# One graph layer pair on one core: the last unit's one-hot rows in its gather buffer, the adjacency sums in five parts over four PSUM banks

## The chip, the core and the metric

The kernel runs on one core of one Trainium2 chip. The metric is the device time of one execution in microseconds; the median of three runs of the kernel before is 566.61 us (565.72 to 568.6).

## What is computed

Two graph layers are applied to x (4096 nodes, 64 features) with an adjacency matrix adj of 4096 x 4096 zeros and ones, about eight ones in a row. Both are pre-norm residual layers:

```
h = relu(layernorm(x))
# layer 0: hyperbolic aggregation over the neighbours j of each node i
log_ij = logmap(h_i, h_j)                 # on the Poincare ball
agg_i  = sum_j adj_ij / deg_i * log_ij
x      = x + expmap(0, agg @ W0 + b0)     # tanh of a norm
# layer 1: the neighbours in order of their column, each weighs half of the next
h   = relu(layernorm(x))
w   = adj * 0.5 ** (k - pos)              # pos: rank of the neighbour in its row
out = x + w @ (h @ W1) + b1
```

## The kernel before

The nodes are 32 blocks of 128 (a partition each). The work has three streams, all written into one list of steps with a due time each (`plan`, filled by `at`, L1454 to L1548); the steps are issued in that order and a list scheduler then fixes the order of the instructions on each engine. [...]

**The adjacency** is loaded block by block (L879, 64 MB in all), transposed on TensorE (L888) and copied by ScalarE as fp8 weights into four `masks` (L891), one for each quarter p of the rows. From them come the candidate lists of each row (`pack`, `search`, `tail_*`), and in place the weights of layer 1 (`step`, L1412).

**Layer 0** goes by 17 units (L1490). Unit n below 16 has two blocks of ordinary neighbour slots (2 x 6 gathers); units 5 to 16 have also a tail: the rows' further neighbours of two or three blocks, three gathers for a block. So unit 16, the last one, has a tail alone (blocks 30 and 31, six gathers). For a unit, `fetch` loads the block's own rows (L1117, L1126), `gather` (L1139) issues one indirect DMA of 128 rows for each slot on GpSimd, `tail_rows` builds one-hot rows (L1156, L1163), transposes them (L1169), copies them (L1170) and selects the target rows by matmuls (L1178). `differ` (L1192 to L1222), `weigh` (L1234 to L1251) and `total` (L1261 to L1288) work out the weighted difference vectors, and the matmuls of L1266 with `total_tail` (L1295) add the tails to y. The tiles of the pool `blk` have one buffer each: the one-hot rows `oh`, the tile `mr` (transposed one-hot rows, target rows, and later the weighted one-hot rows), d and w. So the rows of unit n+1 wait until unit n's total has read `mr`. The gather tile `g` has two buffers.

**Between the layers** `middle` takes five groups of blocks (L846: 8, 8, 8, 6 and 2 blocks) in four stages: stage 0 scales y (L1327 to L1330), stage 1 multiplies by W0 (L1302, L1345), stage 2 does tanh, residual and layernorm (L1353 to L1359, L711 at its end), stage 3 multiplies by W1 and writes the result in three bf16 pieces side by side into `sup` (L1386, L1390, L1403, L1405).

**Layer 1** is the sum over the node blocks: for a part c of the blocks (`sums`, L848) and two row blocks (p, n), `collect` runs one matmul for each node block and row block into a PSUM tile of two halves (L1422, last part also L1430), and adds the tile, whose 192 columns are the three pieces, to `acc`. There are 16 pairs (p, n) for each part. Two ways lead out of PSUM:

- the VectorE way: a reduction over the three pieces (L1441) and one scaled addition to `acc` (L1445)
- the GpSimd way: ScalarE copies the tile to SBUF (L1436, tile `dg` or `mr` in turn by n), and GpSimd adds the three pieces to `acc` one after the other (L1438)

Before, the first part takes the VectorE way, the second and third take the GpSimd way, the last one is split half and half by n. All collects share the two PSUM buffers of `ps_a`. `write` (L1451) sends four blocks of `acc` out after the last part. Part c can start when the groups named in its entry are through stage 3.

```
groups = [(0, 8), (8, 8), (16, 8), (24, 6), (30, 2)]
sums = [(0, 16, (0, 1)), (16, 7, (2,)), (23, 6, (3,)), (29, 3, (4,))]
pool = 0 < c < len(sums) - 1 or (c == len(sums) - 1 and n >= 2)
o = ps_a.tile([P, 2, 2 * P], F32, name="a_ps")
ev = (lst if n % 2 else blk).tile([P, 2, W3], F32, name="dg" if n % 2 else "mr")
```

A dense version of the kernel follows under a condition (L1568) that this input does not meet.

Of the kernel before, what the change touches and what calls it, by code (L numbers as in the profile page):

```python
# [11 lines left out]
F32 = mybir.dt.float32  # L12
BF16 = mybir.dt.bfloat16
# [6 lines left out]
P = 128  # L20
# [36 lines left out]
TB = 3  # L57
MAXT = 3
# [490 lines left out]
def kernel(  # L549
# [34 lines left out]
    nc = tc.nc  # L584
# [4 lines left out]
    DT = D + 1  # L589
# [4 lines left out]
    NSL = 2 * ELL + MAXT * TB  # L594
# [14 lines left out]
    hp_d = dram.tile([P, NB, 3 * DT], BF16, name="hp_d")  # L609
# [6 lines left out]
    with ExitStack() as fast:  # L616
# [174 lines left out]
        late = masks[NQ - 1].bitcast(F32).rearrange("p b c -> p (b c)")  # L791
# [53 lines left out]

        groups = [(0, 8), (8, 8), (16, 8), (24, 6), (30, 2)]  # L846

        sums = [(0, 16, (0, 1)), (16, 7, (2,)), (23, 6, (3,)), (29, 3, (4,))]  # L848


        def bf(at, n):
# [3 lines left out]
        sup, o = [], 0  # L855
# [256 lines left out]
        def fetch(u):  # L1112
            rb = u["ell"]
            if rb is not None:
                hi = blk2.tile([P, 2, DT], F32, name="hi")
                u["hi"] = hi[:, :, 1:DT]
                nc.scalar.dma_start(out=hi, in_=tab_v[:, rb : rb + 2, :])  # L1117
            if u["tail"]:
                t0, nt = u["tail"]

                u["mr"] = blk.tile([P, MAXT * TB, P], F32, name="mr")
                half = u["mr"].rearrange("p b c -> p (b c)").bitcast(BF16)
                u["mt"] = half[:, 0 : MAXT * TB * P].rearrange("p (b c) -> p b c", c=P)
                hr = half[:, MAXT * TB * P :][:, 0 : MAXT * 3 * DT]
                u["hr"] = hr = hr.rearrange("p (b c) -> p b c", c=3 * DT)
                nc.scalar.dma_start(out=hr[:, 0:nt, :], in_=hp_d[:, t0 : t0 + nt, :])  # L1126

        def gather(u):
            rb = u["ell"]
            g = u["g"] = gp.tile([P, NSL, DT], F32, name="g")  # L1130
            idx = []
            if rb is not None:
                idx = [ell_i[:, rb + b, s : s + 1] for b in range(2) for s in range(ELL)]
            u["e2"] = len(idx)
            if u["tail"]:
                t0, nt = u["tail"]
                idx += [tail_i[:, t0 + b, t : t + 1] for b in range(nt) for t in range(TB)]
            for k, i in enumerate(idx):
                nc.gpsimd.indirect_dma_start(  # L1139
                    out=g[:, k, :],  # L1140
                    out_offset=None,
                    in_=tab_d,
                    in_offset=bass.IndirectOffsetOnAxis(ap=i, axis=0),
                )
            u["ns"] = len(idx)

        def tail_rows(u):

            if not u["tail"]:
                return  # L1150
            t0, nt = u["tail"]
            nb = nt * TB
            oh = u["oh"] = blk.tile([P, MAXT * TB, P], BF16, name="oh")

            for k in range(nb):
                nc.scalar.activation(  # L1156
                    oh[:, k, :],
                    row128,
                    AF.Abs,
                    bias=tail_r[:, t0 + k // TB, k % TB : k % TB + 1],  # L1160
                    scale=-1.0,
                )
            nc.scalar.activation(oh[:, 0:nb], oh[:, 0:nb], AF.Relu, bias=1.0, scale=-1.0)  # L1163
            mt, u["sel"] = u["mt"], []
            for k0 in range(0, nb, SEL):
                part = range(k0, min(k0 + SEL, nb))
                mp = ps_m.tile([P, SEL, P], BF16, name="mi")
                for k in part:
                    nc.tensor.transpose(mp[:, k - k0, :], oh[:, k, :], ident_b)  # L1169
                nc.scalar.copy(mt[:, k0 : part.stop], mp[:, 0 : len(part)])  # L1170
            for k0 in range(0, nb, SEL):
                part = range(k0, min(k0 + SEL, nb))
                pool, name = (ps_m, "mi") if k0 else (ps_s, "sel")
                sel = pool.tile([P, SEL, DT], F32, name=name)
                u["sel"].append((k0, part.stop, sel))
                for k in part:
                    for n in range(3):
                        nc.tensor.matmul(  # L1178
                            sel[:, k - k0, :],
                            lhsT=mt[:, k, :],  # L1180
                            rhs=u["hr"][:, k // TB, n * DT : n * DT + DT],
                            start=(n == 0),
                            stop=(n == 2),
                        )
# [68 lines left out]
        def total(u):  # L1253

            d, rb, ns, r = (u[k] for k in ("d", "ell", "ns", "r"))
            e2 = u["e2"]
            if u["tail"]:
                t0, nt = u["tail"]
                mr = u["mr"]
                for k in range(nt * TB):  # L1260
                    nc.scalar.activation(  # L1261
                        mr[:, k, :], u["oh"][:, k, :], AF.Copy, scale=r[:, e2 + k : e2 + k + 1]
                    )
                ag = u["ag"] = ps_s.tile([P, SEL, DT], F32, name="sel")
                for k in range(nt * TB):
                    nc.tensor.matmul(  # L1266
                        ag[:, k // TB, :], lhsT=mr[:, k, :], rhs=d[:, e2 + k, :],
                        start=(k % TB == 0), stop=(k % TB == TB - 1),
                    )
            if not e2:  # L1270
                return
            q, b = divmod(rb, QB)
            if b == 0:
                st["y", q] = yp.tile([P, QB, DT], F32, name="y")

            re = r[:, 0:e2]
            nc.vector.scalar_tensor_tensor(
                re, ell_v[:, rb : rb + 2].rearrange("p b s -> p (b s)"), 0.0, re,
                ALU.is_gt, ALU.mult,
            )  # L1280
            nc.vector.tensor_tensor(d[:, 0:e2], d[:, 0:e2], cols(re, DT), ALU.mult)
            sv = d[:, 0:e2].rearrange("p (b s) c -> p b s c", b=2)
            for dst, one, two in (
                (sv[:, :, 0:3], sv[:, :, 0:3], sv[:, :, 3:6]),
                (sv[:, :, 0:1], sv[:, :, 0:1], sv[:, :, 1:2]),
                (st["y", q][:, b : b + 2, :].unsqueeze(2), sv[:, :, 0:1], sv[:, :, 2:3]),
            ):
                nc.vector.tensor_tensor(dst, one, two, ALU.add)  # L1288
# [124 lines left out]

        def collect(c, p, n):

            pool = 0 < c < len(sums) - 1 or (c == len(sums) - 1 and n >= 2)
            b0, nb, _ = sums[c]
            end = c == len(sums) - 1
            o = ps_a.tile([P, 2, 2 * P], F32, name="a_ps")
            for k in range(2):  # L1420
                for j in range(nb):
                    nc.tensor.matmul(  # L1422
                        o[:, k, 0:W3],
                        lhsT=masks[p][:, b0 + j, bass.ts(2 * n + k, P)],
                        rhs=sup[c][:, j, :],
                        start=(j == 0),
                        stop=(j == nb - 1 and not end),
                    )
                if end:
                    nc.tensor.matmul(  # L1430
                        o[:, k, 0:W3], lhsT=last, rhs=sup[c][:, nb, :], start=False, stop=True
                    )
            ab = acc[:, p * QB + 2 * n : p * QB + 2 * n + 2, :]
            if pool:
                ev = (lst if n % 2 else blk).tile([P, 2, W3], F32, name="dg" if n % 2 else "mr")
                nc.scalar.activation(ev, o[:, :, 0:W3], AF.Copy, scale=2.0**-W8_SHIFT)  # L1436
                for k in range(3):
                    nc.gpsimd.tensor_tensor(ab, ab, ev[:, :, k * D : k * D + D], ALU.add)  # L1438
                return
            red = lst.tile([P, 2, D], F32, name="wsb")  # L1440
            nc.vector.tensor_reduce(  # L1441
                red, o[:, :, 0:W3].rearrange("p k (n c) -> p k c n", n=3), AX.X, ALU.add
            )
            a = ab.rearrange("p k c -> p (k c)")
            nc.vector.scalar_tensor_tensor(  # L1445
                a, red.rearrange("p k c -> p (k c)"), 2.0**-W8_SHIFT, a, ALU.mult, ALU.add
            )
# [8 lines left out]
        def at(when, fn, *args):  # L1456
            plan.append((when, len(plan), fn, args))
# [40 lines left out]
        for n, u in enumerate(units):  # L1498
# [4 lines left out]
            e2 = 2 * ELL if u["ell"] is not None else 0  # L1503
            took = 1.26 * (e2 + (u["tail"][1] * TB if u["tail"] else 0))
            t = start + took
            at(u_fetch, fetch, u)
            at(start, gather, u)
            z = start + SH
            u_fetch = z + 3.0
            at(z, tail_rows, u)  # L1510
            at(z + 1.0, differ, u)
            at(z + 4.0, weigh, u, 0)
            at(z + 5.0, weigh, u, 1)
# [78 lines left out]
```

## Time and profile before

| | us |
|---|---|
| median of the runs | 566.61 |
| the profiled execution | 754.09 |
| its span, first to last instruction | 752.2 |
| last instruction of unit 15's gathers (21 indirect DMAs, from 579.0) | 604.9 |
| y of unit 15 complete (L1295) | 663.83 |
| last piece of `sup` of group 3, of group 4 (L1403) | 697.05, 712.95 |
| first matmul of the last part (L1422) | 723.32 |
| last addition to `acc` on GpSimd (L1438) | 738.98 |

Busy time over the whole span is PE 400.0, VectorE 403.2, ScalarE 345.6 and GpSimd 350.5 us. The granted TensorE clock is 0.668 of full speed in the mean, and 0.9 and more in the last 100 us.

How to read it: a profiled execution is one execution under the profiler, and this one took 187.5 us longer than the median of the runs without it. Times inside it are read from its own span. A row of the groups gives engine, operation and tiles, then busy time, mean duration in ns, idle time just before, and what ended it. In the timeline a row is a start, a duration, an engine and an operation with its count, and the idle time before it in brackets.

### The profile page before, as it was taken

To read this page: it belongs to the slowest core of one execution; us is meant where nothing else is said; L and a number is where in the kernel's file an instruction comes from. 1 tells how busy PE (TensorE), PEld (TensorE's weight loads), DVE (VectorE), ACT (ScalarE), POOL (GpSimd) and SP (SyncE) were. 2 spreads that over 40 slices of the span, in tenths; PEclk is the share of its full clock that TensorE was granted. 3 is DMA by queue.
4 is the path that set the end of the run, shared out by engine and by line. 5 is a ranking of instruction groups with operands and counts; after the bars stand their busy time and mean duration, and the time that the engine had idled before them with its cause. 6 is when DMAs were issued, how large, how long until landed. Compare 5 with 4: busy or idle time off the path is not lost.

```text
span 752.2 us, 11841 instructions
## 1 busy us (share of the span) xinstructions
PE 400.0 (53%) x4094; PEld 344.2 (46%) x4094; DVE 403.2 (54%) x1557; ACT 345.6 (46%) x791; POOL 350.5 (47%) x423
## 2 busy tenths in 40 slices
PE   3742465643632628636067351452274378979881
PEld 3542353532531517535054241342164168979871
DVE  7742386734880518927169463793623136764520
ACT  6742465733842529836156251343242214565430
POOL 1374606246475440562705454587274713007892
PEclk9865576755855757855556555555556669988997
DMA  8994567755963536956201111221111110000001
GB/s 310 384 323 137 192 217 245 261 168 154 343 198 94 180 95 217 322 164 191 33 17 17 29 34 23 44 38 26 30 27 33 28 15 13 14 10 1 2 22 40
DMA packets 42858, 88.23 MB, mean 117 GB/s; under 512 B 14756, under 2 KB 20388, under 8 KB 42660
## 3 DMA queue, kind: packets, MB, share of 16 engines
q1 hardware_dynamic: 21458, 72.93, 26.9%
q0 software_dynamic: 9504, 10.67, 8.1%
q10 hardware_dynamic: 11826, 3.78, 2.3%
q8 instruction: 34, 0.56, 0.3%
q14 instruction: 36, 0.29, 0.1%
HBM read 83.11 MB, written 4.24 MB: 116 GB/s over the span
## 4 chain that ended last, share of the span: by engine, by line
DVE 23%; another core or an unknown queue 22%; PE 20%; ACT 16%; issue 10%; DMA 5%; ACTq 2%; POOL 1%; DVEq 0%; SPq 0%; POOLq 0%
PE a_ps L1422 9%; ACT mask L891 7%; PE a_ps L888 3%; DVE mask L1412 3%; PE words L917 2%; DMA room<-in_adj 2%; DVE cand L981 1%; DVE tl L1095 1%; DVE tb L1093 1%; ACT oh L1156 1%; PE sel L1266 1%; POOL acc L1438 1%; DVE wsb L983 1%; DMA w_sb<-in_L_gnn_weight 1%
## 5 line engine op out<-in xcount | busy, mean ns | idle before, releaser
L1139 POOL DMA_INDIRECT g<-tab_d,ell_i x192 | 198.0, 1031 | 266.2 <-DVE d L1234 84.7
L891 ACT ACTIVATE mask<-a_ps 128x1024 fp8e5<-128x1024 bf16 x128 | 128.2, 1028 | 113.8 <-remote 84.6
L888 PE MATMUL a_ps<-ident_b,room 128*128 128x128 bf16 x1024 | 107.4, 272 | 63.6 <-ACT mask L891 37.4
L1422 PE MATMUL a_ps<-room,mask 128*128 128x192 bf16 x1024 | 109.1, 260 | 32.5 <-issue 25.9
L888 PEld LDWEIGHTS <-room 128*128 128x128 bf16 x1024 | 92.9, 158 | 69.9 <-issue 68.0
L1139 POOL DMA_INDIRECT g<-tab_d,tail_i x96 | 93.8, 977 | 50.8 <-issue 28.1
L1422 PEld LDWEIGHTS <-mask 128*128 128x128 fp8e5 x1024 | 93.1, 104 | 41.1 <-issue 39.3
L917 PEld LDWEIGHTS <-mask 128*128 128x128 fp8e5 x1024 | 49.5, 115 | 107.6 <-ACT mask L891 56.7
L917 PE MATMUL words<-pk,mask 128*128 128x64 bf16 x1024 | 61.1, 219 | 70.2 <-ACT mask L891 44.4
L981 DVE MAX8 cand<-wsb 128x8 f32<-128x256 f32 x96 | 40.5, 422 | 88.5 <-ACT wsb L928 80.8
L1266 PE MATMUL sel<-d,mr 128*128 128x65 f32 x192 | 41.3, 379 | 20.2 <-issue 16.7
L1266 PEld LDWEIGHTS sel<-d,mr 128*128 128x128 f32 x192 | 39.0, 295 | 24.9 <-issue 19.6
L1438 POOL TENSOR_TENSOR acc<-acc,dg 128x128 f32<-128x128 f32 x60 | 28.2, 469 | 36.0 <-ACT dg L1436 33.9
L1412 DVE TENSOR_TENSOR mask<-mask 128x1024 int16<-128x1024 int16 x60 | 40.7, 678 | 6.6 <-ACT q__5085 L1241 4.0
L1441 DVE TENSOR_REDUCE wsb<-a_ps 128x128 f32<-128x384 f32 x24 | 13.3, 555 | 46.0 <-remote 27.8
L1261 ACT ACTIVATE mr<-oh,r 128x128 f32<-128x128 bf16 x96 | 29.3, 389 | 18.0 <-DVE acc L1445 7.5
L1438 POOL TENSOR_TENSOR acc<-acc,mr 128x128 f32<-128x128 f32 x60 | 28.5, 475 | 14.6 <-ACT mr L1436 12.7
L1169 PE MATMUL mi<-ident_b,oh 128*128 128x128 bf16 x96 | 12.6, 283 | 38.1 <-ACT oh L1163 28.2
L904 PE MATMUL words<-gn,ones_b 1*128 1x352 bf16 x32 | 12.3, 390 | 35.1 <-ACT cn L931 20.9
L1156 ACT ACTIVATE oh<-row,tail_r 128x128 bf16<-128x128 bf16 x96 | 29.4, 389 | 3.2 <-DVE tail_r L1109 3.1
L1169 PEld LDWEIGHTS <-oh 128*128 128x128 bf16 x96 | 8.9, 128 | 41.1 <-ACT oh L1163 29.2
L1170 ACT COPY mr<-mi 128x768 bf16<-128x768 bf16 (+1 forms) x20 | 13.5, 674 | 30.6 <-PE mi L1169 12.2
(332 smaller groups left out, 775.1 us busy)
## 6 DMA issues: line engine op xcount, KB each, us to landing
room<-in_adj SPq DMA_DIRECT2D x128, 512.0 KB
g<-tab_d,ell_i POOLq DMA_INDIRECT x192
hp_d<-mask SPq DMA_DIRECT2D x1, 1560.0 KB
g<-tab_d,tail_i POOLq DMA_INDIRECT x96
mr<-hp_d ACTq DMA_DIRECT2D x8, 146.2 KB
tab_d<-mask POOLq DMA_DIRECT2D x2, 520.0 KB
hi<-tab_d ACTq DMA_DIRECT2D x16, 65.0 KB
mask<-in_x SPq DMA_DIRECT2D x2, 512.0 KB
```

What stands on the lines that cost most here:

```text
L888: nc.tensor.transpose(a_ps[:, k, :], upper[:, e : 2 * HC : 2 * JH], ident_b)
L891: nc.scalar.activation(masks[q][:, j0 : j0 + QB, bass.ts(b, P)], a_ps, AF.Copy, scale=2.0**-ONE, saturate=False,)
L917: nc.tensor.matmul(w, lhsT=masks[q][:, j, bass.ts(b, P)], rhs=pk, start=False, stop=True, skip_group_check=True,)
L981: nc.vector.max(out=top, in_=src)
L1139: nc.gpsimd.indirect_dma_start(out=g[:, k, :], out_offset=None, in_=tab_d, in_offset=bass.IndirectOffsetOnAxis(ap=i, axis=0),)
L1156: nc.scalar.activation(oh[:, k, :], row128, AF.Abs, bias=tail_r[:, t0 + k // TB, k % TB : k % TB + 1], scale=-1.0,)
L1169: nc.tensor.transpose(mp[:, k - k0, :], oh[:, k, :], ident_b)
L1261: nc.scalar.activation(mr[:, k, :], u["oh"][:, k, :], AF.Copy, scale=r[:, e2 + k : e2 + k + 1])
L1266: nc.tensor.matmul(ag[:, k // TB, :], lhsT=mr[:, k, :], rhs=d[:, e2 + k, :], start=(k % TB == 0), stop=(k % TB == TB - 1),)
L1412: nc.vector.tensor_tensor(m[:, :, j, :], m[:, :, j, :], m[:, :, j - 1 if j else JH - 1, :], ALU.add)
L1422: nc.tensor.matmul(o[:, k, 0:W3], lhsT=masks[p][:, b0 + j, bass.ts(2 * n + k, P)], rhs=sup[c][:, j, :], start=(j == 0), stop=(j == nb - 1 ...
L1438: nc.gpsimd.tensor_tensor(ab, ab, ev[:, :, k * D : k * D + D], ALU.add)
```

## The change

Three things are changed.

1. `sums` has five parts in place of four: the first part of 16 blocks is cut into one of 7 (it needs group 0 alone) and one of 9 (groups 0 and 1 are then there; its entry names group 1).
2. `collect` takes its PSUM tile from `ps_a` for even n and from `ps_w` (the two buffers of the tile `words`) for odd n, so it has four buffers. The parts from the third on take the GpSimd way for odd n and the VectorE way for even n; the first two take the VectorE way. `ev` is written as before, so with n odd it is always the tile `dg` of the pool `lst`, which has one buffer.
3. The last unit (the one without ordinary slots) takes its gather tile already in `fetch`, and its one-hot rows, their transposes and the target rows lie in the part of that tile that its six gathers do not write. Its `fetch` and `tail_rows` are due 2.0 and 4.5 us after the previous unit's `tail_rows` (due time `before`), and not after its total. Its selected rows go to the PSUM tile `mi` and not `sel`. `mr` is taken in `total` for the weighted rows alone.

```diff
-        sums = [(0, 16, (0, 1)), (16, 7, (2,)), (23, 6, (3,)), (29, 3, (4,))]
+        sums = [(0, 7, (0,)), (7, 9, (1,)), (16, 7, (2,)), (23, 6, (3,)), (29, 3, (4,))]
...
                 t0, nt = u["tail"]
+                if rb is None:
+
+                    u["g"] = gp.tile([P, NSL, DT], F32, name="g")
+                    nb = nt * TB
+                    left = u["g"][:, nb:, :].rearrange("p s c -> p (s c)").bitcast(BF16)
+                    u["mt"] = left[:, 0 : nb * P].rearrange("p (b c) -> p b c", c=P)
+                    u["oh"] = left[:, nb * P : 2 * nb * P].rearrange("p (b c) -> p b c", c=P)
+                    hr = left[:, 2 * nb * P :][:, 0 : nt * 3 * DT]
+                    u["hr"] = hr = hr.rearrange("p (b c) -> p b c", c=3 * DT)
+                    nc.scalar.dma_start(out=hr, in_=hp_d[:, t0 : t0 + nt, :])
+                    return
...
-            g = u["g"] = gp.tile([P, NSL, DT], F32, name="g")
+            if rb is not None:
+                u["g"] = gp.tile([P, NSL, DT], F32, name="g")
+            g = u["g"]
...
-            oh = u["oh"] = blk.tile([P, MAXT * TB, P], BF16, name="oh")
+            if u["ell"] is not None:
+                u["oh"] = blk.tile([P, MAXT * TB, P], BF16, name="oh")
+            oh = u["oh"]
...
-                pool, name = (ps_m, "mi") if k0 else (ps_s, "sel")
+                pool, name = (ps_m, "mi") if k0 or u["ell"] is None else (ps_s, "sel")
...
-                mr = u["mr"]
+                mr = u.get("mr")
+                if mr is None:
+                    mr = blk.tile([P, MAXT * TB, P], F32, name="mr")
...
-            pool = 0 < c < len(sums) - 1 or (c == len(sums) - 1 and n >= 2)
+            late = c >= 2 and n % 2 == 1
...
-            o = ps_a.tile([P, 2, 2 * P], F32, name="a_ps")
+            pool, name = (ps_w, "words") if n % 2 else (ps_a, "a_ps")
+            o = pool.tile([P, 2, 2 * P], F32, name=name)
...
-            if pool:
+            if late:
                 ev = (lst if n % 2 else blk).tile([P, 2, W3], F32, name="dg" if n % 2 else "mr")
...
-            at(u_fetch, fetch, u)
+            at(u_fetch if u["ell"] is not None else before + 2.0, fetch, u)
             at(start, gather, u)
             z = start + SH
             u_fetch = z + 3.0
-            at(z, tail_rows, u)
+            at(z if u["ell"] is not None else before + 4.5, tail_rows, u)
+            before = z
```

## The prediction

> **What bounds the kernel now.** I read the page's slices first, then the groups of the last 92 us, then the timeline there, then the chain of waits.
>
> The profiled execution took 754.09 us (span 752.2), the median run 566.61, so 187.5 us of the profile are not in a plain run. The timeline shows where they may lie: while GpSimd issues a unit's gathers, other engines nearly stop.
>
> ```profile
> 271.54 0.95 POOL L1139 DMA_INDIRECT g<-tab_d,tail_i  x1 [0.30 <-issue]
> 272.79 0.95 POOL L1139 DMA_INDIRECT g<-tab_d,tail_i  x1 [0.31 <-issue]
> 277.06 1.02 ACT L891 ACTIVATE mask<-a_ps 128x1024 fp8e5<-128x1024 bf16 x1 [20.43 <-remote]
> ```
>
> A gather starts every 1.25 us, 288 x 1.25 = 360 us in all, and ScalarE stood 20.43 us for no engine of the trace. I assume that these stops are the profiler's. After 604.9 us only six gathers are left, so the end of the profile is carried over one to one, and before that I treat the gathers as the pace of a plain run.
>
> The end is GpSimd's. Its digits in the last slices are 7 8 9 2, and the groups from 660 us on show why:
>
> ```profile
> L1438 POOL TENSOR_TENSOR acc<-acc,mr 128x128 f32<-128x128 f32 x60 | 28.5, 475 | 14.6 <-ACT mr L1436 12.7
> L1438 POOL TENSOR_TENSOR acc<-acc,dg 128x128 f32<-128x128 f32 x60 | 28.2, 469 | 36.0 <-ACT dg L1436 33.9
> L1436 ACT ACTIVATE dg<-a_ps 128x384 f32<-128x384 f32 x20 | 9.8, 491 | 8.6 <-POOL acc L1438 6.1 <-PE a_ps L1422 1.3 <-PE a_ps L1430 1.2
> L1441 DVE TENSOR_REDUCE wsb<-a_ps 128x128 f32<-128x384 f32 x9 | 5.0, 557 | 15.6 <-PE a_ps L1430 15.2
> ```
>
> 40 collects on the GpSimd way are 120 additions. From 678.05 to 738.98 it does 117 of them. ScalarE's copies wait for GpSimd, TensorE waits for the copies:
>
> ```profile
> 714.63 0.49 ACT L1436 ACTIVATE mr<-a_ps 128x384 f32<-128x384 f32 x1 [1.19 <-POOL acc L1438]
> 715.18 2.14 PE L1422 MATMUL a_ps<-room,mask 128*128 128x192 bf16 x24 [0.36 <-ACT mr L1436]
> 715.50 0.99 POOL L1438 TENSOR_TENSOR acc<-acc,mr 128x128 f32<-128x128 f32 x2
> 715.58 0.49 ACT L1436 ACTIVATE dg<-a_ps 128x384 f32<-128x384 f32 x1 [0.45 <-POOL acc L1438]
> ...
> 717.35 0.49 ACT L1436 ACTIVATE mr<-a_ps 128x384 f32<-128x384 f32 x1 [1.28 <-PE a_ps L1422]
> ```
>
> Two collects take 2.72 us (714.63 to 717.35), 1.36 each, because the additions of two tiles are mixed and none waits for its predecessor. Alone, three dependent additions of one tile took longer:
>
> ```profile
> 693.28 1.52 POOL L1438 TENSOR_TENSOR acc<-acc,mr 128x128 f32<-128x128 f32 x3 [0.57 <-ACT mr L1436]
> ```
>
> Before that, from unit 13's total to unit 15's, TensorE is full: the stretch 605.00 to 663.80 has 54.21 us of PE work, and the chain of waits gives 54% of 600 to 665 us to the collects of L1422 (11 x 32 matmuls stand between these totals).
>
> **What the Trainium skill says.** "Perfetto Trace Analysis", Matmuls: independent groups should rotate through PSUM banks so that evacuation overlaps the next group. The trace agrees that banks are short, but it is small: from 660 us L1422 idled 6.3 us in all for evacuations, under GpSimd's pace. "TensorEngine Tiling (Array Packing)", PSUM Bottleneck: use both ScalarE and VectorE to evacuate. The trace before has VectorE idle in 678 to 724 (18.1 of 46 us busy). "GPSIMD Engine Reference", 3.1: an elementwise add is about twice as slow as on VectorE; here 0.47 against 0.29 us (128x130, L1288), so the rule holds with a smaller factor. "SBUF — State Buffer", two separate sides: VectorE and GpSimd share a port as an exclusive lock. Agrees in part: three additions took 1.83 us at 678.05 beside VectorE work, and 1.52 alone.
>
> **The change part by part.** Zero is unit 15's y (663.83); the span ends at +88.4, GpSimd at +75.2. The order of the changed program's instructions gives what stands where; durations are from rows of the trace before.
>
> *Two ways in turn, four banks.* After zero there are 48 collects in both kernels. Before, 40 by GpSimd; after, 24 by GpSimd (72 additions, 48 removed) and 24 by VectorE (16 more). But an odd n always takes `dg`, with one buffer: ScalarE's copy waits for the third addition of the copy before. One pass is 0.49 + 0.08 (copy to first addition, 693.20 to 693.28) + 1.52 + 0.03 (709.83 to 709.86) = 2.12 us in place of 1.36. 24 x 2.12 = 50.9 us against 40 x 1.36 = 54.4: the work that looks like 40% less is 6% less in line. TensorE needs 28 x 0.083 = 2.3 us for a pair of collects of the third part, 24 x 0.083 = 2.0 of the fourth, 16 x 0.083 = 1.33 of the last, so the passes set the pace in the last two parts.
>
> The last two parts (16 passes) can't start before group 3's `sup`, +33.2 before. In the new order on ScalarE the second half of group 2's `sup`, unit 16's weights and its six scalings stand ahead of group 3's first copy: y ready +3.3, r of unit 16 +8.0, three scalings to +9.0, copy to +9.6, three more to +10.5, copy, one `dg`, then the square of group 3, so its norm is at +13.5 (before 671.79, +8.0). From there to the end of L711 14.1 us before; six collects now stand in it on VectorE, 6 x (0.55 + 0.29) = 5.0, of which about 3 fall in waits for ScalarE (1.74 us before L731 alone): 16.2, +29.7 (before +22.1). `sup` then took 11.1 with 54 collect matmuls in between; they are gone in the new order: 11.1 - 54 x 0.083 + 0.6 for a copy in the way = 7.2, `sup` at +36.9. The fourth part's first copy stands behind group 4's exponential, +39.7. 16 passes are 33.9, and ScalarE's queue stops them about 2.4 us for group 4's layernorm: end at +76.1 against +75.2, so +0.9. In other words GpSimd's load goes, and what is late next is one buffer. Output DMA and end (13.2) stay. The four banks themselves I cost at nothing: the 6.3 us of TensorE's waits lay under GpSimd's pace, and one of the two new ones is held by `middle` from L1345 to L1356 (about 7 us, twice); if banks had been the limit, up to -6.3.
>
> *First part in two.* 224 matmuls move ahead of group 1, to units 10 and 11, and all 32 collects of the first two parts (16 more than before, 16 x 0.84 = 13.4 us of VectorE) are over before unit 15's differences. In unit 15 this removes three collects from the line of L1208 to L1251 (648.63, 651.52, 656.20: 3 x 0.84) and half a microsecond of waits for TensorE: -3 us if TensorE had done the rest under the gathers. If TensorE binds as in the profile, 352 matmuls between the totals become 180, 172 x 0.0855 = 14.7, less 2 to 3 for more collects on VectorE in unit 14 and 2.7 for the new rows: -9.5. I take -5, nearer the first, since a gather of 26.3 us (21 x 1.25) covers most of a unit in a plain run. Of the 16 moved collects nine stand ahead of the reduction that frees unit 11's `g` (7.6 us of VectorE), seven ahead of unit 12's (5.9); the other buffer's gathers (26.3 us) hide them; without that cover it is up to +13.5. I take +1.
>
> *Last unit's rows.* Removed after zero: six one-hot rows, Relu, transposes, copy, 18 matmuls, one DMA (661.9 to 668.6). These ran beside group 3's stage 0, and unit 16's y at 677.5 waited for group 3 anyway (group 4's transposes at 691), so the gain is nothing, and its weights now come ahead of group 3 (in the sum above). Moved: 6 x 0.31 + 0.84 = 2.7 us and the 97.5 KB load go on ScalarE's queue between unit 14's signs and its logarithm; the load's issue waits until unit 14's reduction has freed `g`, and unit 14's weights stand behind it. Bound 0 (gathers of unit 15 hide it) to 3.9; it is in the -9.5 case, else 0. GpSimd's and SP's queues keep their order.
>
> Sum: +0.9 - 5 + 1 = -3.1, 566.61 - 3.1 = 563.5. In the profile the TensorE case would show more, 752.2 + 0.9 - 9.5 + 1 = 744.6 of span, 746.5 with the 1.9 us around it, against its own 754.09.
>
> **Rivals.**
> - *TensorE binds between the totals in plain runs too*: for it the 54.21 of 58.8 us; against it the gathers. +0.9 - 9.5 = 558.
> - *The single `dg` buffer decides (slower)*: place, the parts after group 3's `sup`. If VectorE's share of the port lengthens a pass from 2.12 to 2.43 (1.83 for three additions, seen at 678.05), 16 passes cost 5 more, and another 2.5 us of `sup` in VectorE's queue give 563.5 + 7.5 = 571. It decides once passes and `sup` take 3.1 us more together, a pass of 2.31. Against it: in the last part VectorE mostly reads PSUM.
> - *Collects hold the gathers that follow units 11 and 12*: between nine and all sixteen uncovered, +7.6 to +13.5 in place of +1, so 570 to 576; I take 573. For it: VectorE had 64.7 of 100 us of work from 400 to 500 us.
> - *It doesn't do what it says*: collects move, but each lands where it hid before: 566.6.
>
> **How the numbers follow.** About 0.5% (2.8 us) can be told from no change. Forecast case 0.40 (559 to 568, half of it faster, most of the rest same), TensorE case 0.20, `dg` 0.23, gathers held 0.10, nothing 0.07. Faster 0.20 + 0.20 = 0.40; same 0.17 + 0.07 + 0.02 = 0.26; slower 0.34. The range from 555 to 574 takes in all five with 2 to 3 us of room at the fast end; forecast's own, 559 to 568.
>
> **What would show it.** Right: `dg` copies spaced 2.1 us in the last part, waiting for GpSimd; collects of the first part before unit 12; none between unit 14's and 15's totals; group 3's norm about 13 us after unit 15's y. Wrong: additions of the last part with no wait for the buffer, `sup` of group 3 before +34, or gathers after units 11 and 12 that wait longer for VectorE.

## The result: slower by 0.8 %

| | median, us | against the kernel before |
|---|---|---|
| before (20 runs) | 566.57 | 1 |
| after (20 runs) | 571.22 | 1.008 (1.0056 to 1.0104) |

The ratio leaves disturbed runs out, here and below, so it can differ a little from the quotient of two medians.

The profiled execution of after took 570.47 us (span 568.7). The profile of before had 754.09, so the two can't be laid side by side as a whole. A second profile of the kernel before (b_again below) took 569.41 us, and in it the end runs as in the first: from unit 15's y, group 3's norm comes at +8.0, the last piece of its `sup` at +33.3, GpSimd's last addition at +75.3. Carrying the end over one to one was right. It is the profile of before in all that follows.

First the end of after, 477 us to 568.7. A row is line, engine, operation, tiles and count, then busy us and mean ns, then idle time before it and what ended it:

```profile
L1456 POOL TENSOR_TENSOR acc<-acc,dg 128x128 f32<-128x128 f32 x72 | 33.9, 471 | 62.2 <-ACT dg L1454 58.5
...
L1459 DVE TENSOR_REDUCE wsb<-a_ps 128x128 f32<-128x384 f32 x24 | 13.3, 554 | 8.2 <-PE a_ps L1440 5.6 <-PE a_ps L1448 2.2
L1454 ACT ACTIVATE dg<-words 128x384 f32<-128x384 f32 x24 | 11.8, 491 | 32.7 <-POOL acc L1456 22.4 <-PE words L1440 7.3 <-PE a_ps L1440 2.8
```

GpSimd has 72 additions instead of 120 and is idle nearly as long as it works: 33.9 us of work, and of the 62.2 us of idle time 31.4 lie before the first addition, 30.8 between the others. It waits for ScalarE's copy, and the copy waits for GpSimd (22.4 us): that is one buffer going back and forth. The timeline of the last part of after shows the pass (start, duration, engine, operation, in brackets the idle time before it):

```profile
541.38 0.49 ACT L1454 ACTIVATE dg<-words 128x384 f32<-128x384 f32 x1 [1.63 <-POOL acc L1456]
...
541.94 1.52 POOL L1456 TENSOR_TENSOR acc<-acc,dg 128x128 f32<-128x128 f32 x3 [0.60 <-ACT dg L1454]
...
543.50 0.49 ACT L1454 ACTIVATE dg<-words 128x384 f32<-128x384 f32 x1 [1.63 <-POOL acc L1456]
```

The next copy starts 2.12 us after this one, the forecast to the hundredth. From the copy at 521.41 to the last addition at 556.28, the 16 passes took 34.9 us (forecast 33.9 + 2.4).

Where the steps of the two kernels lie, in us. The first three columns count from the first gather of unit 12 (347.8 in the second profile of before, 345.1 in after), since the gathers keep nearly one pace in both (unit 16's first comes 109.2 and 107.5 us after unit 12's); the rest count from unit 15's y:

| | norm of group 1 | `sup` of group 2 ends | y of unit 15 | norm of group 3 | `sup` of group 3 | last addition |
|---|---|---|---|---|---|---|
| before | 26.9 | 132.2 | 132.0 | +8.0 | +33.3 | +75.3 |
| after | 39.7 | 137.5 | 131.8 | +16.6 | +39.9 | +79.5 |
| forecast for after | as before | as before | 128 | +13.5 | +36.9 | +76.1 |

Two things are off. Unit 15's y came no earlier, and group 3's norm came 3.1 us later than forecast; all that follows it is late by that. And a thing that the forecast never priced stands at the left: group 1's norm is 12.8 us later.

TensorE's timeline of after around that norm shows why. Group 1's transposes (L1319) and its multiplication by W0 (L1351, L1362) are in one queue with the collects of the first part (L1440):

```profile
366.12 0.63 PE L1319 MATMUL o<-ident,y 128*64 128x128 f32 x4 [1.83 <-DVE y L1347]
...
368.39 2.40 PE L1440 MATMUL a_ps<-room,mask 128*128 128x192 bf16 x14 [0.34 <-DVE wsb L1459]
373.13 2.07 PE L1351 MATMUL words<-w1n_b,room 1*128 1x512 f32 x2 [2.34 <-DVE wsb L1459]
...
377.03 2.42 PE L1440 MATMUL a_ps<-room,mask 128*128 128x192 bf16 x14
379.24 1.81 PE L1440 MATMUL words<-room,mask 128*128 128x192 bf16 x10
380.98 1.37 PE L1362 MATMUL words<-w_sb,room 64*128 64x64 f32 x8
```

A collect's matmuls wait for a PSUM buffer, the buffer waits for VectorE's reduction, and the group's matmuls stand behind; L1351, which takes a `words` buffer as the odd collects now do, waits 2.34 us for such a reduction itself. VectorE has other work between the reductions: in its timeline from 355 to 382.8 us no idle time is noted. Its collects of that stretch stand between the steps of a list search (L1093, L1095):

```profile
374.41 0.53 DVE L1459 TENSOR_REDUCE wsb<-a_ps 128x128 f32<-128x384 f32 x1
...
375.84 0.53 DVE L1459 TENSOR_REDUCE wsb<-words 128x128 f32<-128x384 f32 x1
...
377.18 0.53 DVE L1459 TENSOR_REDUCE wsb<-a_ps 128x128 f32<-128x384 f32 x1
```

Theory: the split puts 14 collects (13 in my expectations, miscounted) on VectorE ahead of group 1's norm; they delay groups 1 and 2, and through the common queues unit 15's y and group 3. The one buffer is a second, separate loss. Rivals: the early rows of unit 16 hold group 3; the two ways in turn are the loss; the split's matmuls, not VectorE, make the delay.

### The profile page after: what moved, and what is told of

Its sections match the earlier page's. It is cut to its first block, busy times and chain, and to the rows that moved or that the text cites. A ratio compares the mean times of both kernels' runs of the same rounds, so it can differ in the third digit from the quotient of the medians.

```text
span 568.7 us, 11838 instructions
## 1 busy us (share of the span) xinstructions
PE 386.2 (68%) x4094; PEld 336.5 (59%) x4094; DVE 421.4 (74%) x1621; ACT 335.7 (59%) x775; POOL 341.7 (60%) x375
## 3 DMA queue, kind: packets, MB, share of 16 engines
q0 software_dynamic: 9504, 10.67, 10.2%
## 4 chain that ended last, share of the span: by engine, by line
POOL 25%; PE 22%; DVE 16%; DMA 14%; issue 10%; ACT 9%; ACTq 1%; DVEq 0%; POOLq 0%; SPq 0%
POOL g L1152 21%; PE a_ps L1440 5%; PE words L1440 4%; DMA g<-tab_d,ell_i 4%; DMA g<-tab_d,tail_i 3%; POOL acc L1456 3%; PE sel L1283 2%; ACT mask L891 2%; PE t L1403 2%; DMA tab_d<-mask 2%; PE t L1407 2%; PE o L1319 1%; DMA w_sb<-in_L_gnn_weight 1%; DVE cand L981 1%; DMA tl_d<-tl 1%
## 5 line engine op out<-in xcount | busy, mean ns | idle before, releaser
L1152 POOL DMA_INDIRECT g<-tab_d,ell_i x192 | 206.8, 1077 | 101.8 <-issue 54.9
L891 ACT ACTIVATE mask<-a_ps 128x1024 fp8e5<-128x1024 bf16 x128 | 127.7, 1032 | 17.5 <-PE a_ps L888 15.7
L888 PE MATMUL a_ps<-ident_b,room 128*128 128x128 bf16 x1024 | 102.1, 263 | 33.1 <-ACT mask L891 16.7
L1152 POOL DMA_INDIRECT g<-tab_d,tail_i x96 | 96.4, 1004 | 29.3 <-issue 27.4
L1440 PEld LDWEIGHTS <-mask 128*128 128x128 fp8e5 x1024 | 93.1, 105 | 11.7 <-issue 9.5
L1456 POOL TENSOR_TENSOR acc<-acc,dg 128x128 f32<-128x128 f32 x72 | 33.9, 471 | 62.2 <-ACT dg L1454 58.5
L1440 PE MATMUL a_ps<-room,mask 128*128 128x192 bf16 x512 | 58.0, 265 | 3.5 <-DVE wsb L1459 2.5
L1440 PE MATMUL words<-room,mask 128*128 128x192 bf16 x512 | 56.3, 257 | 3.5 <-ACT dg L1454 3.1
L1283 PE MATMUL sel<-d,mr 128*128 128x65 f32 x192 | 36.7, 352 | 24.8 <-ACT mr L1278 24.8
L1237 ACT ACTIVATE g<-d 128x1344 f32<-128x1344 f32 (+3 forms) x17 | 19.1, 1122 | 24.0 <-DVE d L1207 9.8
L1454 ACT ACTIVATE dg<-words 128x384 f32<-128x384 f32 x24 | 11.8, 491 | 32.7 <-POOL acc L1456 22.4
L1459 DVE TENSOR_REDUCE wsb<-a_ps 128x128 f32<-128x384 f32 x40 | 22.0, 551 | 9.1 <-PE a_ps L1440 6.4
L904 PE MATMUL words<-gn,ones_b 1*128 1x352 bf16 x32 | 11.7, 371 | 22.5 <-ACT cn L931 20.1
L983 DVE MATCH_REPLACE8 wsb<-cand,wsb 128x256 f32<-128x256 f32 x64 | 26.3, 411 | 0.0
```

The source lines that it names most:

```text
L888: nc.tensor.transpose(a_ps[:, k, :], upper[:, e : 2 * HC : 2 * JH], ident_b)
L891: nc.scalar.activation(masks[q][:, j0 : j0 + QB, bass.ts(b, P)], a_ps, AF.Copy, scale=2.0**-ONE, saturate=False,)
L983: nc.vector.match_replace(out=src, in_to_replace=top, in_values=src, imm_value=0.0)
L1152: nc.gpsimd.indirect_dma_start(out=g[:, k, :], out_offset=None, in_=tab_d, in_offset=bass.IndirectOffsetOnAxis(ap=i, axis=0),)
L1283: nc.tensor.matmul(ag[:, k // TB, :], lhsT=mr[:, k, :], rhs=d[:, e2 + k, :], start=(k % TB == 0), stop=(k % TB == TB - 1),)
L1440: nc.tensor.matmul(o[:, k, 0:W3], lhsT=masks[p][:, b0 + j, bass.ts(2 * n + k, P)], rhs=sup[c][:, j, :], start=(j == 0), stop=(j == nb - 1 ...
```

## The experiments

**b_again**: the kernel before, unchanged, once, with a profile.

> The kernel before, unchanged, for a second profile. If the stops of the first profile (754 us) were the profiler's, this one shows about 567 us, with gathers of a unit following each other without long gaps from 230 us on. Theory (the end got longer, the stretch up to unit 15's y did not get shorter): y of unit 15 within 2 us of the changed kernel's 476.8, and 88 us from it to the end of the span. Rival (the first part in two pushed the units back, by collects on VectorE or rows on ScalarE): y of unit 15 at 472 or earlier, so that the end is as long as in the changed kernel. If the recorded gain of 5 us came: y at about 481.

569.41 us, y of unit 15 at 479.8, 87.9 us from there to the end. The y is 3.0 us later than in after (476.8), more than the 2 us of the theory, but 2.7 of them are there at unit 12's first gather already. Against these gathers the y is as early as in after (132.0, 131.8), which says neither of gain nor of push alone. e17 below, the kernel before in all but one buffer of the last parts, has 130.7. One profile each leaves differences of one or two us here open.

**e1, two buffers**, and **e3, four parts**, each in the changed kernel (ratios of this series against 565.46 us):

```diff
-ev = (lst if n % 2 else blk).tile([P, 2, W3], F32, name="dg" if n % 2 else "mr")
+ev = (lst if n // 2 else blk).tile([P, 2, W3], F32, name="dg" if n // 2 else "mr")
```

> The changed kernel with one edit: the GpSimd way takes its tile from two buffers in turn (n = 1 mr, n = 3 dg) in place of dg alone. Theory (one buffer sets the pace of the last two parts): two tiles' additions mix, a pass takes 3 x 0.47 = 1.4 us where TensorE lets it (a pair of collects of the fourth part is 2.0 us of TensorE, of the last 1.33), so about 1.7 in the mean in place of 2.12, 16 passes are 6 to 7 us shorter: 564 to 566. Rival (the loss lies ahead of the last two parts, in the units or in group 3's way): no more than 2 us, 569 or more.

```diff
-sums = [(0, 7, (0,)), (7, 9, (1,)), (16, 7, (2,)), (23, 6, (3,)), (29, 3, (4,))]
+sums = [(0, 16, (0, 1)), (16, 7, (2,)), (23, 6, (3,)), (29, 3, (4,))]
...
-late = c >= 2 and n % 2 == 1
+late = c >= 1 and n % 2 == 1
```

> The changed kernel with the four parts of before (16, 7, 6, 3), the first by VectorE, the others in turn by both. Theory (under the gathers the place of the first part's matmuls costs nothing): 569.5 to 572.5. If the recorded 5 us had come from the split: 574 to 577. If the split had cost (collects of units 10 to 12 ahead of the reductions that free a gather buffer): 566 or less.

e1: 566.34 us, 1.0014 (0.9986 to 1.0043). All up to `sup` of group 3 is as in after (+40.0), the last addition comes at +74.9 and not at +79.5. So the one buffer costs 4.6 us in the profile, 0.0066 or 3.7 us in the ratios, less than the 6 to 7 I expected. e3: 566.11 us, 1.0017 (0.9995 to 1.0039). This was a miss: I expected nothing, the split costs 0.0063 or 3.6 us. In its profile group 1's norm is back at 28.1, `sup` of group 2 at 126.8, y of unit 15 at 130.6, group 3's norm at +12.4, the last addition at +74.9.

**e2, rows late**, the changed kernel without the early rows (`fetch`, `gather`, `tail_rows`, `total` and the due times as before):

```diff
-at(u_fetch if u["ell"] is not None else before + 2.0, fetch, u)
+at(u_fetch, fetch, u)
...
-at(z if u["ell"] is not None else before + 4.5, tail_rows, u)
+at(z, tail_rows, u)
```

> The changed kernel without its third item: the last unit's rows, load and due times as before. Theory (unit 16's weights and scalings now stand ahead of group 3 in the queues, so its norm came at +16.6 us after unit 15's y and not at +8): group 3's norm 4 to 6 us earlier, its last piece of sup 3 to 5 us earlier, 566 to 569 in all. Rival (group 4 is what waits, and the early rows feed it): group 4 comes 3 us later, 571 to 574.

569.3 us, 1.0081 (1.005 to 1.0112), as after. Group 3's norm came no earlier (+17.4), so the early rows are not what holds it.

**e4 to e11: two series in another condition.** These were the runs that should have settled the split. The kernels: e4 and e8 have the edits of e1 and e3 together; e5 and e9 are the kernel before with the five parts alone; e6 and e10 leave the first part's sums out of `acc`; e7 and e11 let the first part wait for the second.

```diff
# e6, e10 (and e13): in collect, ahead of the reduction
+if c == 0:
+    nc.vector.tensor_copy(acc[:, p * QB + 2 * n : p * QB + 2 * n + 2, 0:1], o[:, :, 0:1])
+    return
# e7, e11: in the pairs' due times
-(max([ready[m] for m in sums[c][2]] + [made[p]]), c, p)
+(max([ready[m] for m in sums[max(c, 1)][2]] + [made[p]]), c, p)
```

> The changed kernel with both edits of the first set: the four parts of before, and two buffers in turn on the GpSimd way. Theory (two separate losses: the split delays the way of groups 1 and 2 to unit 15, one buffer sets the pace of the last parts): both come back, 1.0017 - 0.0066 = 0.995 of the kernel before, about 563. Rival (the last parts are held by one thing that each edit relieves alone): as either edit alone, 1.001 to 1.003.

> The kernel before with the five parts alone (first two by VectorE, third and fourth by GpSimd, last half and half, two PSUM buffers, rows of the last unit as before). Theory (16 more collects on VectorE at 340 to 450 us, 13 of them ahead of group 1's norm, delay groups 1 and 2 and through them unit 15 and the start of the GpSimd way): slower by 3 to 6 us, ratio 1.005 to 1.01. The recorded step (-5, +1 for the units): 562 to 563, ratio 0.993. Rival (the split costs only together with the two ways in turn): 1.000.

> The changed kernel in which the 16 collects of the first part do not add to acc: VectorE copies one column of each half (256 values) instead of the reduction and the scaled addition; matmuls, order and due times stay. Theory (VectorE's time in these collects, 0.84 us each and 13.4 us in all, makes the delay): group 1's norm comes 6 to 10 us earlier against the gathers, ratio 1.001 to 1.004. Rival (the 224 matmuls of the first two parts, or the order itself, make it): 1.006 to 1.009.

> The changed kernel in which the collects of the first part are due only when the second part is (after group 1): the same 32 collects on VectorE, 4 and not 13 of them ahead of group 1's norm. Theory A (their place ahead of group 1 makes the delay): most of 3.6 us comes back, ratio 1.002 to 1.004. Theory B (their number does, wherever they stand before unit 15): 1.006 to 1.010.

> The kernel of e4 once more. In the series of e4 to e7 every run of the kernel before took about 754 us and not 566, with the stops at the gathers that its first profile has; if this series is at 566, the numbers are of the condition of the first result. Theory (two separate losses): 0.995, about 563. Rival (one thing that each edit relieves alone): 1.001 to 1.003.

> The kernel of e5 once more, for the condition of 566 us. Theory (16 more collects on VectorE ahead of unit 15, 13 of them ahead of group 1's norm): 1.004 to 1.010, the start of the GpSimd way 3 to 5 us later against the gathers. The recorded step (-4): 0.993. Rival (the split costs only together with the two ways in turn): 1.000.

> The kernel of e6 once more (the first part's sums are left out of acc, one column is copied in their place), for the condition of 566 us. Theory (VectorE's 13.4 us of these collects delay groups 1 and 2): group 1's norm 6 to 10 us earlier against the gathers of unit 12 than in the changed kernel, ratio 1.001 to 1.004. Rival (matmuls or the order itself): 1.006 to 1.009.

> The kernel of e7 once more (the first part is due only with the second, after group 1; 4 collects and not 13 ahead of group 1's norm), for the condition of 566 us. Theory A (their place ahead of group 1): 1.002 to 1.004. Theory B (their number, wherever they stand before unit 15): 1.006 to 1.010.

| | median, us | before in that series | ratio |
|---|---|---|---|
| e4, e8 | 752.58, 752.57 | 754.13, 753.42 | 0.9938 (0.9906 to 0.9969), 1.0115 (1.0021 to 1.0208) |
| e5, e9 | 770.2, 770.06 | 754.13, 753.42 | 1.023 (1.0166 to 1.0293), 1.0324 (1.0252 to 1.0396) |
| e6, e10 | 769.89, 768.11 | 754.13, 753.42 | 1.0203 (1.0147 to 1.0259), 1.0295 (1.0194 to 1.0395) |
| e7, e11 | 774.05, 777.12 | 754.13, 753.42 | 1.0259 (1.0195 to 1.0324), 1.0356 (1.0216 to 1.0496) |

The kernel before took 754 us in these series, so they don't answer for 566. What they show for their own condition: every kernel with the split is 15 to 24 us slower in the medians, whatever its reads cost, and those without it are level with before in the medians (their two ratios contradict each other). Why the split costs so much more there, and why e6 doesn't help, stays open; so does e7's question, the place of the collects against their number, which no series at 566 us has answered.

**e12 to e14: the same edits, in a series at 565.72 us.**

> Four parts as before and two buffers in turn, a third time, for the condition of 566 us. Theory (two separate losses): ratio 0.993 to 0.997, about 563; the GpSimd way ends 78 us after unit 15's y in the changed kernel's way less 4.6 less 5.3, so at +70. Rival (one thing that each edit relieves alone): 1.001 to 1.003.

> The changed kernel with the sums of the first part left out of acc (VectorE copies one column in their place), a third time, for the condition of 566 us. Theory (VectorE's time in these 16 collects): group 1's norm 6 to 10 us earlier against the gathers of unit 12, ratio 1.001 to 1.004. Rival (the matmuls or the order of the queues, since each of these collects still stands ahead of group 1 and waits for TensorE): norm within 3 us of the changed kernel's, ratio 1.006 to 1.009.

> The kernel before with the five parts alone, a third time, for the condition of 566 us. Theory (the split delays groups 1 and 2, and sup of group 2 starts the GpSimd way): 1.004 to 1.010. The recorded step (-4): 0.993. Rival (the split costs only together with the two ways in turn): 1.000.

e12 (both edits): 561.3 us, 0.9921 (0.9883 to 0.9958), faster than both kernels. The losses add up: 1.008 - 0.0066 - 0.0063 = 0.9951 was to be expected, within its interval. With two buffers the last part goes, in its steady stretch from 528.02 to 533.30, at TensorE's pace:

```profile
530.66 0.49 ACT L1454 ACTIVATE dg<-words 128x384 f32<-128x384 f32 x1 [0.83 <-PE words L1448]
...
531.98 0.49 ACT L1454 ACTIVATE mr<-words 128x384 f32<-128x384 f32 x1 [0.83 <-PE words L1448]
...
533.30 0.49 ACT L1454 ACTIVATE dg<-words 128x384 f32<-128x384 f32 x1 [0.83 <-PE words L1448]
```

A copy every 1.32 us, waiting for matmuls and no more for GpSimd; this is the 1.33 us of a pair of collects in the last part that the forecast had worked out.

e13 (the first part's reads cut from 0.84 to 0.15 us of VectorE, matmuls and order kept): 566.36 us, 0.9994 (0.9971 to 1.0017), still faster than the 1.001 to 1.004 of the theory. Group 1's norm is at 29.0 in place of 39.7. So VectorE's time in these collects, with the PSUM buffers that it holds meanwhile, makes group 1 late, not the matmuls, and without it the loss is gone in the sum. TensorE's timeline of e13 at the same place:

```profile
365.60 0.63 PE L1319 MATMUL o<-ident,y 128*64 128x128 f32 x4 [1.12 <-DVE y L1347]
366.07 1.32 PE L1440 MATMUL words<-room,mask 128*128 128x192 bf16 x14
367.32 1.10 PE L1362 MATMUL words<-w_sb,room 64*128 64x64 f32 x8
368.35 0.63 PE L1319 MATMUL o<-ident,y 128*64 128x128 f32 x4
371.11 1.96 PE L1362 MATMUL words<-w_sb,room 64*128 64x64 f32 x8 [2.13 <-ACT room L1320]
```

The collect is still ahead of the group's matmuls, but it doesn't wait; the group's second half starts at 371.11 and not at 380.98, 9.6 us earlier against unit 12's gathers (344.8 and 345.1). The end, though, doesn't come back the way that the theory has it. Unit 15's y is at 129.2 (131.8 in after), while the tail behind it stays late: group 3's norm at +15.0 and the last addition at +78.2, where e3, without the split, has +12.4 and +74.9.

e14 (before with five parts alone): 569.46 us, 1.007 (1.0036 to 1.0103). The split loses by itself, without the two ways in turn. In its timeline TensorE waits at the same place:

```profile
368.25 1.50 PE L1423 MATMUL a_ps<-room,mask 128*128 128x192 bf16 x14 [3.88 <-DVE wsb L1442]
```

Group 1's norm is at 39.2. Unit 15's y is as in before (132.0), and group 3's norm (+10.2) and the last addition (+77.2) are 2 us later: the split gained nothing where I had put its gain. And group 1 hands nothing on here: group 2's norm is at 97.8 (99.2 in before, 105.4 in after) and its `sup` ends at 131.7 (132.2 in before). The split costs 4 us all the same, so the chain from group 1 over group 2 to the end, as the theory has it, is not shown.

What the theory left out, and the kept traces show, is the clock that TensorE was granted around unit 15's y (matmuls are counted as far as the traces have them):

| | matmuls between the y's of units 14 and 15 | us between these y's | granted clock there | granted clock from 12 us before unit 15's y to 10 us after it |
|---|---|---|---|---|
| before (b_again) | 260 | 22.5 | 1.00 | 0.99 |
| e3, four parts | 247 | 20.7 | 1.00 | 1.00 |
| after | 99 | 21.5 | 0.53 | 0.50 |
| e13 | 116 | 21.3 | 0.50 | 0.58 |
| e14 | 112 | 20.4 | 0.70 | 0.62 |

The other kernels with four parts in this condition (e12, e15, e16, e17) have 1.00 in the last column, the other two with five (e1, e2) 0.50. With the first part's collects gone from this place, TensorE has gaps in after, and the last matmuls ahead of y go slower than the same ones in e3 (second fence):

```profile
458.92 0.82 PE L1184 MATMUL mi<-ident_b,oh 128*128 128x128 bf16 x6 [3.63 <-ACT oh L1178]
...
472.84 3.94 PE L1283 MATMUL sel<-d,mr 128*128 128x65 f32 x18
```

```profile
472.19 2.15 PE L1283 MATMUL sel<-d,mr 128*128 128x65 f32 x18
```

The granted clock of after is 1.00 from 452 to 455 us, 0.78 to 458, and 0.50 from there to 485; TensorE works 0.29 of the 3 us from 455 to 458. In the 10 us after y it is busy throughout in both kernels, with 45 matmuls in after and 116 in e3. By the ratio of the two lines (3.94 to 2.15) these 10 us of after would be about 5.5 at the clock of e3, an estimate; group 3's norm is 4.2 us later than there. So the slower clock is enough to account for the lateness behind y. That the gaps bring the clock down, and how much of the split's loss is the clock's and how much VectorE's, no run tests.

**e15 and e16: the two steps recorded as worth nothing**, in e12's kernel; **e17: the buffer's price in the kernel before** (series at 565.66 us):

```diff
# e15: e12 with e2's edit
# e16: e12 with two PSUM buffers
-pool, name = (ps_w, "words") if n % 2 else (ps_a, "a_ps")
+pool, name = ps_a, "a_ps"
# e17: the kernel before with
-ev = (lst if n % 2 else blk).tile([P, 2, W3], F32, name="dg" if n % 2 else "mr")
+ev = lst.tile([P, 2, W3], F32, name="dg")
```

> The kernel of e12 (four parts, two buffers in turn) with the last unit's rows, load and due times as before. The recorded step (rows early gain nothing, since group 4 waits for group 3 anyway): as e12, ratio 0.991 to 0.994. Rival (early rows free the queues of ScalarE and TensorE behind unit 15's y): 0.996 to 0.999. Other rival (unit 16's weights ahead of group 3 hold its norm): 0.986 to 0.990.

> The kernel of e12 with all collects in the two PSUM buffers of ps_a, as before, in place of four. The recorded step (four banks are worth nothing under GpSimd's pace): as e12, 0.991 to 0.994. Rival (with GpSimd's pace gone, TensorE's waits for an evacuation show: about 0.3 us for each of 24 collects of the last parts): 0.999 to 1.003.

> The kernel before with one edit: all 40 collects of the GpSimd way take the one buffer dg, none mr. Theory (a pass with one buffer is 2.12 us whatever stands around it): 39 passes of 2.12 are 82.7 us from the first copy to the last, against 70.6 in the kernel before (482.1 to 552.7), so 12 us slower, ratio 1.018 to 1.024. Rival (the pace is GpSimd's or TensorE's own): 1.000 to 1.005.

e15: 560.64 us, 0.9925 (0.9898 to 0.9952); e16: 560.57 us, 0.9898 (0.9874 to 0.9921). Neither differs from e12 (0.9921) by more than the intervals. So the early rows and the other two banks are worth nothing that can be told, each taken alone. By elimination the gain of these three kernels, 0.8 to 1.0 %, is the rest: VectorE taking each second collect, with two buffers on the other way, which is the advice of the Trainium skill, "TensorEngine Tiling (Array Packing)", PSUM Bottleneck, to evacuate with both engines. e17: 581.66 us, 1.0313 (1.0271 to 1.0354), 17.7 us slower by one name. Its timeline, from the fourth part of the sums:

```profile
539.62 0.49 ACT L1436 ACTIVATE dg<-a_ps 128x384 f32<-128x384 f32 x1 [1.63 <-POOL acc L1438]
...
540.19 1.52 POOL L1438 TENSOR_TENSOR acc<-acc,dg 128x128 f32<-128x128 f32 x3 [0.60 <-ACT dg L1436]
541.74 0.49 ACT L1436 ACTIVATE dg<-a_ps 128x384 f32<-128x384 f32 x1 [1.63 <-POOL acc L1438]
```

The same 2.12 us, in each of the last 20 passes. I expected 12 us in all: 39 passes took 89.1 us (475.9 to 565.0), 2.28 each and not 2.12, since earlier ones take up to 3.9. What holds those, the layernorms of `middle` perhaps, was not looked into.

## Why the prediction was wrong

Forecast 563.5, measured 571.2. The 7.7 us are one step, and it is the second:

- *Two ways in turn, four banks (+0.9).* Right. e3 is this step without the split: 1.0017, +1.0 us, with the last addition at +74.9. The pass (2.12), the 16 passes (34.9 for 36.3), the banks at nothing (e16) all held. What I took as a plain term of the sum was worth an edit, though: 3.7 us (e1).
- *First part in two (-5, and +1 for units 11 and 12).* This is what failed: -4 on record, +3.6 us by e3 and +4.0 by e14 (0.007 x 565.72). The -5 supposed that fewer collects between unit 14's and unit 15's totals bring y forward; it came at 131.8 after unit 12's gathers against 132.0. With 99 matmuls in place of 260 the stretch between the two y's was only 1.0 us shorter, and the clock granted in it was 0.53 and not 1.00. The +1 asked only whether the moved collects hold the gathers. They don't: in after the gathers of units 13 to 16 start 1.2 to 1.4 us after the last one of the unit before. But I didn't ask who else stands behind VectorE there: group 1's norm does, and comes 12.8 us later. Nor did I ask how fast TensorE is in the place that the collects leave. `sup` of group 2 is 5.3 us later, the first copy of the third part comes 14.1 us after unit 15's y (in e3 0.2 us), and group 3's norm follows. Of the 3.4 us that the end was later than forecast (+79.5 and +76.1 at the last addition), 3.1 are there at the norm already (+16.6 for +13.5): the tail's error is the split's as well, since in e3 the norm is at +12.4. The forecast reckoned a collect's matmul at 0.083 us throughout; in b_again 32 in a row took 2.80 us at a clock of 1.00 (from 457.02, 0.088 each), in e14 21 took 3.21 us at 0.52 (from 479.17, 0.153 each). Which way the loss takes stays open. e13 shows that VectorE's time in the moved collects is worth about all of it, e14 that it need not pass through group 2, and in both the tail is late and the clock low.
- *Last unit's rows (0).* Right, by e2 and e15.
- *The 187.5 us are the profiler's.* Wrong: the kernel before took as long in whole series without this (e4 to e11). For the end that did no harm, for the units it did. In the 40 us from unit 12's first gather, VectorE has 31.8 us of work in that profile and 37.0 in the one at the pace of the runs, 3 us of room and not 8, before any collect is moved there.

Of the rivals, the one with the single buffer gave 571, but by a longer pass (2.43) and a later `sup` in VectorE's queue; the pass did not lengthen, so its number is luck. The one with the gathers (573) had the right collects and the right engine and the wrong thing waiting for them. TensorE binding between the totals (558) is out: the split alone, which should have shown it, lost, though TensorE was busy for 22.5 of the 22.6 us between the two y's in b_again. A full engine is not yet the one that sets the time.

## What to carry to other kernels

Work moved "under" a bound stream is free only for those who wait for that stream: list what else stands in the queues that it is moved into (here group 1, 12.8 us later), and look at what the place that it leaves becomes: here TensorE had gaps there, and its granted clock was 0.50 where it had been 0.99 (12 us before unit 15's y to 10 us after it). A hand-over through one buffer costs the sum of both sides (0.49 + 1.52 + 0.11 us here) and not the longer of them; when halves of the work are dealt out by parity, see that the buffers are not dealt out by the same parity. And before a profile is read for what hides where, compare its own time with that of the runs.

## What was not expected of the hardware

The same program ran at two paces, about 566 us and about 754 us, each kept through whole series of runs. At the second the engines stop while GpSimd issues gathers. The page's row of ScalarE's copies to `masks` in b_again (569.41 us):

```profile
L891 ACT ACTIVATE mask<-a_ps 128x1024 fp8e5<-128x1024 bf16 x128 | 127.9, 1032 | 21.5 <-PE a_ps L888 19.5
```

and in e4 (profiled at 746.45 us):

```profile
L891 ACT ACTIVATE mask<-a_ps 128x1024 fp8e5<-128x1024 bf16 x128 | 128.4, 1027 | 107.7 <-remote 85.9
```

The copies are as fast as ever (1027 and 1032 ns), but ahead of them the engine stood 107.7 us and not 21.5, most of it for nothing that the trace names. In the first profile of the kernel before (754.09 us) it is 113.8 us, 84.6 of them so. A gather is no slower either (L1152 in e4 1037 ns in the mean, L1139 in b_again 1088). What stops the engines was not found, and no run was made for it.
